# One written order for the dense experts and a two-expert chain after the attention, in place of the scheduler's

## The chip, the cores and the metric

The kernel runs on one core of a Trainium2 chip. The metric is the time of the device for one execution, in microseconds (us); the numbers before are the median of three runs and one profiled execution. TensorE is called PE below (its weight loads PEld), VectorE DVE, ScalarE ACT, GpSimd POOL; SP (SyncE) issues most of the transfers. Each engine carries out its own instructions in the order in which they stand in its queue, and waits on semaphores for the others.

## The reference, cut to what matters

The input x has 4 batches of 1024 tokens with 128 features. The network has four layers with residuals: causal softmax attention with 16 heads, a mixture of experts, linear attention with 16 heads of width 8, and the same mixture of experts again. Each layer's input is normalised first.

```python
x = x + attention_a(_layernorm(x), Wq, Wkv, Wo, bo)     # softmax, 16 heads of 64
x = x + ffn(_layernorm(x), router_w, expert_weights)
x = x + attention_b(_layernorm(x), ...)                 # cumulative sums, 16 heads of 8
x = x + ffn(_layernorm(x), router_w, expert_weights)
# ffn: 32 experts of 128x128, the two best of each token
rw = softmax(x @ router_w.T)
vals, idx = top_k(rw, 2)
w_masked = zeros_like(rw).at[tokens, idx].set(vals)
out = sum(x_flat * w_masked[:, e:e+1] @ W[e] for e in range(32))
```

All of it is in float32.

## The kernel before, in words

All tokens stay in `x_sb`, as 32 row blocks of 128 tokens (8 for each batch). The attention phase runs over batches and pairs of heads, in an order that is written out by hand (`tc.manual_schedule()` keeps the order of the program on each engine).

The mixture of experts is computed in two ways. The **two-expert chain** (`experts`, a Python generator that is advanced a piece at a time) does a whole batch sparsely: router, places by prefix sums, a scatter of the tokens' scaled rows into a buffer in DRAM (`xs_d`, indirect DMA from POOL), per group of four experts a load, transposes, matmuls and a store (`ys_d`), and then 16 gathers from DRAM (`fetch`, L449). Scatters and gathers are put in a `queue`, from which the caller takes one at a time. The chains of batches 0 to 2 run beside the attention; the last pieces of batch 2's, its 16 gathers, are left over at the attention's end. The **dense way** computes for a row block all 32 experts: 8 matmuls `pe` of 128x512 (L922), each with four experts, from the 32 resident weights `we_sb`. Of the 8 results, five are scaled and added to `x_sb` by DVE (20 instructions at L937), three (`ACT_GROUPS`) are scaled by ACT into tiles `t` (L930), which POOL adds up (L944 to L946), and DVE adds the sum (L871, in `settle`). The router's weights `w` (L892 to L912) come before: normalise, transpose, copy `xnT`, logits `pl`, softmax, two maxima, `match_replace`.

After the attention there are three stages. **Stage f** is the dense way for the last 8 row blocks (`moe("f", ...)`, two quads of four), and beside it `fill` advances the gathers that are left and `prepare(0)` and `prepare(1)`, the features of the linear attention for the first 8 row blocks (statistics, POOL's `nb_l`, ACT's `xn_l`, transposes, four projections `pj`, Exp, Sigmoid, Ln). The **linear attention** (`lin`) goes over 32 row blocks: POOL makes the products `kv`, PE sums them cumulatively (`cumulate`, `carry`), DVE multiplies and reduces (`m`, `num`), and PE projects; `ahead` advances the next `prepare`. **Stage s** is the dense way for row blocks 8 to 31 (six quads of four), and beside it `pieces` advances the chain for batch 0.

In stages f and s nothing fixes the order by hand: there the framework's scheduler decides it, from priorities and its costs, and may also draw instructions of a later stage forward between those of the linear attention, which has a written order of its own:

```python
        if turn[0] in (4, 18):
            preps.append(prepare(len(preps), pool))
        if turn[0] % 2:
            for p in preps:
                next(p, None)
```

In the dense way of before the whole router of a quad stands in the program ahead of that quad's matmuls, and `between` (that is `fill` or `pieces`) is called once before each matmul. There are 5 PSUM banks for `pe` and 3 for everything else.

Of the kernel before, what the change touches and what calls it, by code (L numbers as in the profile page):

```python
# [20 lines left out]
def hybrid_kernel(  # L21
# [107 lines left out]

    def normed_T(pool, xnp, c0, n, nm, known=None):  # L130

        mv, rstd = known or statistics(c0, n, nm)
        xn = xnp.tile([P, n, D], F32, tag=f"xn{n}", bufs=8 // n, name=f"xn_{nm}")
        xnT = xnp.tile([P, n * P], F32, tag=f"xnT{n}", name=f"xnT_{nm}")
        for c in range(n):
            nc.vector.tensor_scalar(
                xn[:, c, :], x_sb[:, c0 + c, :], mv[:, c, 0:1], rstd[:, c : c + 1],
                ALU.subtract, ALU.mult,
            )
        for g in range(0, n, 4):  # L140
            pt = pool.tile([P, 512], F32, tag="ps1", name=f"pxn_{nm}_{g}")
            for c in range(4):
                nc.tensor.transpose(pt[:, c * P : (c + 1) * P], xn[:, g + c, :], ident)
            nc.scalar.copy(xnT[:, g * P : (g + 4) * P], pt)
        return xnT
# [711 lines left out]
    TB = 12  # L857
    ACT_GROUPS = (1, 4, 6)

    def moe(nm_, store, first=0, between=None, known=(), lag=0):  # L860
        with ExitStack() as ph:
            xnp = ph.enter_context(tc.tile_pool(name=f"xnp{nm_}", bufs=2, reuse_waits="tile"))
            mp = ph.enter_context(tc.tile_pool(name=f"mp{nm_}", bufs=3, reuse_waits="tile"))
            ps_1 = ph.enter_context(tc.tile_pool(name=f"mps1{nm_}", bufs=3, space=PSUM, reuse_waits="tile"))
            ps_e = ph.enter_context(tc.tile_pool(name=f"mpse{nm_}", bufs=5, space=PSUM, reuse_waits="tile"))
            due = []

            def settle(keep):
                while len(due) > keep:
                    xs, s, done = due.pop(0)  # L870
                    nc.vector.tensor_tensor(xs, xs, s[:, :D], ALU.add)  # L871
                    if store and done is not None:
                        b, r = divmod(done, NB)
                        nc.sync.dma_start(
                            out=out_v[b, :, r : r + 4, :], in_=x_sb[:, done : done + 4, :]
                        )

            for q in range(first, NT // 4):
                nm = f"{nm_}_{q}"
                c0 = q * 4  # L880
                xnT = normed_T(
                    ps_1, xnp, c0, 4, f"m{nm}", known[q - first] if known else None
                )
                pl = ps_1.tile([P, 512], F32, tag="ps1", name=f"pl_{nm}")
                for c in range(4):
                    nc.tensor.matmul(
                        pl[:, c * E : (c + 1) * E], xnT[:, c * P : (c + 1) * P], rwT,
                        start=True, stop=True,
                    )
                plv = pl[:, : 4 * E].rearrange("p (c e) -> p c e", c=4)  # L890
                mx = small.tile([P, 4], F32, tag="mx", name=f"mx_{nm}")
                nc.vector.tensor_reduce(mx, plv, AX.X, ALU.max)  # L892
                ex = mp.tile([P, 4, E], F32, tag="ex", name=f"ex_{nm}")
                nc.vector.tensor_tensor(
                    ex, plv, mx.unsqueeze(2).to_broadcast([P, 4, E]), ALU.subtract
                )
                nc.scalar.activation(ex, ex, AF.Exp)
                sm = small.tile([P, 4], F32, tag="sm", name=f"sm_{nm}")
                nc.vector.tensor_reduce(sm, ex, AX.X, ALU.add)
                nc.vector.reciprocal(sm, sm)  # L900
                tp, rwx = top[q % 2]
                nc.vector.tensor_tensor(
                    rwx[:, :, 0:E], ex, sm.unsqueeze(2).to_broadcast([P, 4, E]), ALU.mult
                )
                m8 = small.tile([P, 4, 8], F32, tag="m8", name=f"m8_{nm}")
                for c in range(4):
                    nc.vector.max(m8[:, c, :], rwx[:, c, 0:E])
                nc.vector.tensor_copy(tp[:, :, 0:2], m8[:, :, 0:2])
                w = mp.tile([P, 4, E + 6], F32, tag="w", name=f"w_{nm}")
                for c in range(4):  # L910
                    nc.vector.match_replace(w[:, c, :], tp[:, c, :], rwx[:, c, :], 0.0)
                nc.vector.tensor_tensor(  # L912
                    w[:, :, 0:E], rwx[:, :, 0:E], w[:, :, 0:E], ALU.subtract
                )
                for c in range(4):
                    xs = x_sb[:, c0 + c, :]
                    parts = []
                    for g in range(E // 4):
                        if between:
                            between(ps_1)  # L920
                        pe = ps_e.tile([P, 512], F32, tag="e", name=f"pe_{nm}_{c}_{g}")
                        nc.tensor.matmul(  # L922
                            pe, xnT[:, c * P : (c + 1) * P],
                            we_sb[:, 4 * g : 4 * g + 4, :].rearrange("p e d -> p (e d)"),
                            start=True, stop=True,
                        )
                        if g in ACT_GROUPS:
                            t = mp.tile([P, 512], F32, tag="t", bufs=TB, name=f"t_{nm}_{c}_{g}")
                            for e in range(4):
                                nc.scalar.mul(  # L930
                                    t[:, e * D : (e + 1) * D], pe[:, e * D : (e + 1) * D],
                                    w[:, c, 4 * g + e : 4 * g + e + 1],
                                )
                            parts.append(t)
                        else:
                            for e in range(4):
                                nc.vector.scalar_tensor_tensor(  # L937
                                    xs, pe[:, e * D : (e + 1) * D],
                                    w[:, c, 4 * g + e : 4 * g + e + 1], xs,
                                    ALU.mult, ALU.add,  # L940
                                )
                    s = parts[0]
                    for t in parts[1:]:
                        nc.gpsimd.tensor_tensor(s, s, t, ALU.add)  # L944
                    nc.gpsimd.tensor_tensor(s[:, :256], s[:, :256], s[:, 256:], ALU.add)
                    nc.gpsimd.tensor_tensor(s[:, :D], s[:, :D], s[:, D : 2 * D], ALU.add)  # L946
                    due.append((xs, s, c0 if c == 3 else None))
                    settle(lag)
            settle(0)


# [96 lines left out]
    def fill(pool):  # L1048

        banks[0] = pool  # L1050
        turn[0] += 1
        if turn[0] in (4, 18):
            preps.append(prepare(len(preps), pool))
        if turn[0] % 2:
            for p in preps:
                next(p, None)
        elif turn[0] > 8:
            if queue:
                queue.pop(0)()
            for e in list(sides):  # L1060
                if next(e, "end") == "end":
                    sides.remove(e)

    turn, preps = [0], []
    moe("f", False, NT // 4 - 2, fill, known)
    for p in preps:
        for _ in p:
            pass
    assert not (sides or queue) and len(preps) == 2

    with lin as ph:

        ph.enter_context(tc.manual_schedule())
        lp = ph.enter_context(tc.tile_pool(name="lp", bufs=3))
        ps_c = ph.enter_context(tc.tile_pool(name="ps_c", bufs=1, space=PSUM))
        ps_n = ph.enter_context(tc.tile_pool(name="ps_n", bufs=1, space=PSUM))
        ps_1 = ph.enter_context(tc.tile_pool(name="ps_l", bufs=4, space=PSUM))
        AHEAD = 26

        def products(u):  # L1080

            kq, va = feats[u // G]
            k = kq[:, u % G, :P]
# [72 lines left out]
        def ahead(third):  # L1156
# [5 lines left out]
            for r in list(running):  # L1162
                if next(r, "end") == "end":
                    running.remove(r)

        kv = products(0)
        ends = []
        for u in range(NT + 4):
# [9 lines left out]
            if u < NT:  # L1178
                carry(u, kv)
                f = finish(u, m)  # L1180
                next(f)
                ends.append(f)
                kv = nkv
            ahead(3 * u + 2)

    def pieces(pool):

# [43 lines left out]
```

## Time and profile before

| what | before |
|---|---|
| runs | 2033.25 us median of 3 (2030.45 to 2037.73) |
| profiled execution: its own time | 2037.51 us |
| profiled execution: span from first to last instruction | 2035.8 us |
| mean granted PE clock | 0.975 |
| PE busy | 1890.7 us (93%) |
| DVE busy | 1482.9 us (73%) |
| ACT busy | 1234.6 us (61%) |
| POOL busy | 1139.5 us (56%) |
| DMA | 62.54 MB moved |

The page gives the busy time of each engine, the span in 40 slices with the busy share in tenths, and groups of instructions by source line. The trace is also read in stretches of time (busy time of each engine, granted clock, DMA share), as waits (who waited for whom) and as a timeline. Busy shares are averages over stages with different limits, so a stage is read from its own stretch.

### The profile page before, as it was taken

The numbers are of one execution on the slowest core, as the hardware profiler recorded it, in microseconds if no ns is written. First come the engines' busy times: TensorE is split into PE (matmuls) and PEld (weight loads), VectorE is DVE, ScalarE is ACT, GpSimd is POOL, SyncE is SP. The second block draws the span as 40 slices with busy tenths as digits, with TensorE's granted clock in tenths as the row PEclk, the third lists the DMA queues.
The fourth block names the chain that finished last, engine by engine and source line by source line (L and its number), as shares of the span: only waits on it lengthen the run. The fifth ranks groups of instructions, "written<-read, shape, count | busy, mean of one in ns | idle before, by whom it ended". The sixth has DMA issues, their size and how long they took to land.

```text
span 2035.8 us, 33636 instructions
## 1 busy us (share of the span) xinstructions
PE 1890.7 (93%) x10066; PEld 1052.5 (52%) x10066; DVE 1482.9 (73%) x4467; ACT 1234.6 (61%) x3889; POOL 1139.5 (56%) x2080
## 2 busy tenths in 40 slices
PE   6999999999999999999999999999958898987898
PEld 3555555555555655555565555556633454543443
DVE  5777776776787677778767676777547678966788
ACT  4766666676677566766766676776526466334344
POOL 3444445444665476556745854675476566655644
PEclk9999999999999999999999999999979999997999
DMA  7000000000003310000131100003230000004300
GB/s 214 1 1 1 1 1 1 1 1 1 1 13 93 92 22 10 1 1 5 54 107 45 18 1 1 1 17 111 80 82 0 0 0 1 0 1 123 101 11 11
DMA packets 111875, 62.54 MB, mean 31 GB/s; under 512 B 5552, under 2 KB 110160, under 8 KB 111568
## 3 DMA queue, kind: packets, MB, share of 16 engines
q1 hardware_dynamic: 101936, 50.43, 8.7%
q0 software_dynamic: 9472, 8.40, 2.1%
q8 instruction: 82, 1.34, 0.3%
q10 hardware_dynamic: 288, 1.57, 0.2%
q14 instruction: 97, 0.79, 0.1%
HBM read 35.60 MB, written 24.77 MB: 30 GB/s over the span
## 4 chain that ended last, share of the span: by engine, by line
PE 64%; DVE 12%; ACT 10%; POOL 9%; issue 3%; DMA 1%; ACTq 0%; SPq 0%; POOLq 0%; DVEq 0%
PE s L598 19%; PE po L704 10%; PE pt L687 10%; PE pe_s L922 6%; DVE nmx L607 5%; ACT p L632 3%; PE pw L719 3%; PE pk L547 3%; POOL x_sb L449 2%; ACT pT L691 2%; PE pe L430 2%; PE pv L561 2%; PE cum L1103 1%; ACT p L637 1%; PE pe_f L922 1%
## 5 line engine op out<-in xcount | busy, mean ns | idle before, releaser
L607 DVE TENSOR_REDUCE nmx<-s 128x2 f32<-128x1024 f32 x512 | 604.5, 1219 | 218.5 <-PE s L598 217.8
L632 ACT ACTIVATE p<-s,nmx 128x512 f32<-128x512 f32 (+3 forms) x640 | 361.2, 575 | 311.8 <-DVE nmx L607 264.5
L598 PE MATMUL s<-kT,qT 64*128 64x512 f32 x2048 | 518.0, 619 | 8.0 <-ACT p L632 4.5
L674 POOL TENSOR_SCALAR p<-p,f,ri 128x512 f32<-128x512 f32 (+3 forms) x768 | 503.8, 673 | 0.9 <-issue 0.6
L687 PEld LDWEIGHTS pt<-ident,p 128*128 128x128 f32 x2304 | 249.9, 141 | 219.1 <-issue 91.1
L687 PE MATMUL pt<-ident,p 128*128 128x128 f32 x2304 | 335.9, 282 | 24.4 <-POOL rs L652 7.1
L691 ACT COPY pT<-pt 128x512 f32<-128x512 f32 (+3 forms) x768 | 324.4, 510 | 11.9 <-PE pt L687 9.6
L656 POOL TENSOR_TENSOR rs<-rs,f 128x2 f32<-128x2 f32 x256 | 52.1, 204 | 438.5 <-ACT f L623 409.1
L704 PE MATMUL po<-pT,va 128*64 128x256 f32 (+1 forms) x2560 | 291.1, 365 | 0.6 <-DVE oT L711 0.6
L598 PEld LDWEIGHTS s<-kT,qT 64*128 64x128 f32 x2048 | 173.3, 185 | 195.4 <-issue 94.2
L637 ACT ACTIVATE p<-s,nmx 128x128 f32<-128x128 f32 x512 | 180.7, 366 | 107.3 <-DVE nmx L607 104.6
L704 PEld LDWEIGHTS po<-pT,va 128*64 128x64 f32 x2560 | 167.0, 136 | 97.2 <-issue 32.6
L922 PE MATMUL pe_s<-we_sb,xnT_ms 128*128 128x512 f32 x384 | 186.4, 630 | 22.9 <-DVE x_sb L937 16.4
L937 DVE SCALAR_TENSOR_TENSOR x_sb<-pe_s,w_s,x_sb 128x128 f32<-128x128 f32 x480 | 141.4, 343 | 19.2 <-PE pe_s L922 14.6
L645 DVE SCALAR_TENSOR_TENSOR p<-p,qtri 128x128 f32<-128x128 f32 x512 | 144.9, 310 | 7.0 <-ACT p L637 3.9
L652 POOL TENSOR_TENSOR rs<-rs 128x2 f32<-128x2 f32 x192 | 43.9, 229 | 186.7 <-DVE ri L665 186.7
L632 ACT ACTIVATION_READ_ACCUMULATOR p<-s,nmx 128x1 f32 x640 | 139.0, 217 | 0.0
L930 ACT ACTIVATE t_s<-pe_s,w_s 128x128 f32<-128x128 f32 x288 | 82.2, 369 | 92.5 <-PE pe_s L922 75.5
L922 PEld LDWEIGHTS pe_s<-we_sb,xnT_ms 128*128 128x128 f32 x384 | 72.2, 199 | 116.3 <-issue 37.4
L944 POOL TENSOR_TENSOR t_s<-t_s,t_s 128x512 f32<-128x512 f32 x48 | 60.9, 1269 | 81.4 <-ACT t_s L930 81.1
L724 DVE TENSOR_TENSOR x_sb<-pw,x_sb 128x128 f32<-128x128 f32 x128 | 36.9, 289 | 79.8 <-PE pw L719 79.7
L719 PE MATMUL pw<-wo_sb,oT 128*128 128x128 f32 x512 | 84.5, 289 | 1.8 <-DVE x_sb L724 1.0
(302 smaller groups left out, 2669.5 us busy)
## 6 DMA issues: line engine op xcount, KB each, us to landing
xs<-xs_d SPq DMA_DIRECT2D x33, 256.0 KB, 3.1
ys_d<-ys SPq DMA_DIRECT2D x33, 256.0 KB, 2.4
we<-_ffn_expert_weights_dram SPq DMA_DIRECT2D x24, 256.0 KB, 3.6
xs_d<-zero SPq DMA_DIRECT2D x2, 3008.0 KB, 17.9
we<-_ffn_expert_weights_dram SPq DMA_DIRECT2D x45, 64.0 KB, 1.8
xs_s<-xs_d SPq DMA_DIRECT2D x11, 256.0 KB, 3.6
ys_d<-ys_s SPq DMA_DIRECT2D x11, 256.0 KB, 3.4
we_sb<-_ffn_expert_weights_dram SPq DMA_DIRECT2D x4, 512.0 KB, 6.0
```

The source lines that it names most:

```text
L598: nc.tensor.matmul(st[:, h, :], self.qT[rows, self.ib * P : (self.ib + 1) * P], self.kT[rows, j * 512 : (j + 1) * 512], start=True, stop=True,
L607: nc.vector.tensor_reduce(self.nmx[:, i, :], self.s[i], AX.X, ALU.max, negate=True)
L632: nc.scalar.activation(self.p[h][:, at : at + m * P], self.s[i][:, h, : m * P], AF.Exp, bias=bias, accum_out=self.rs[:, i, h : h + 1],)
L637: nc.scalar.activation(self.p[h][:, at + m * P : at + (m + 1) * P], self.s[i][:, h, m * P : (m + 1) * P], AF.Exp, bias=bias,)
L645: nc.vector.scalar_tensor_tensor(d, d, 1.0, qtri, ALU.mult, ALU.mult, accum_out=self.rs[:, 2, h : h + 1])
L674: nc.gpsimd.tensor_scalar(w, w, self.f[:, i, h : h + 1], self.ri[:, h : h + 1], ALU.mult, ALU.mult,)
L687: nc.tensor.transpose(pt[:, c * P : (c + 1) * P], self.p[h][:, (g + c) * P : (g + c + 1) * P], ident,)
L691: nc.scalar.copy(self.pTs[h][:, g : g + m, self.col : self.col + P], pt[:, : m * P].rearrange("p (c i) -> p c i", c=m),)
L704: nc.tensor.matmul(po[h * DH : (h + 1) * DH, c0:256], va[:, jb, h, :], pTs[h][:, jb, c0:], start=(jb == 0), stop=(jb == n - 1),)
L719: nc.tensor.matmul(pw[:, :P], oTs[i][:, c * P : (c + 1) * P], wo_sb[:, pr, :], start=(i == 0), stop=(i == len(prs) - 1),)
L922: nc.tensor.matmul(pe, xnT[:, c * P : (c + 1) * P], we_sb[:, 4 * g : 4 * g + 4, :].rearrange("p e d -> p (e d)"), start=True, stop=True,)
L937: nc.vector.scalar_tensor_tensor(xs, pe[:, e * D : (e + 1) * D], w[:, c, 4 * g + e : 4 * g + e + 1], xs, ALU.mult, ALU.add,)
```

## The change

`moe` and `normed_T` go, and two functions take their place. `routed` is a generator that gives a quad's statistics, normalisation, transposes, logits and routing weights in small pieces, and leaves `xnT` and `w` in `ready`. `dense` goes over the quads; after each matmul and its scaling it advances the router of the *next* quad by one piece and calls `beside(turn)`. From the attention's end on everything is under `manual_schedule`, so the order of the program is the order on each engine. POOL's adds of the scaled tiles stand directly after the second and third tile, and DVE adds a block's sum while it is at matmul 3 of the third block after it (`settle(2)`).

Beside stage f, `fill` advances `prepare(0)` and `prepare(1)` in turn and takes one gather in each four matmuls; while the router of the first quad is written, `prepare(0)` is advanced a piece for each of its pieces. The router of stage s's first quad is written into the last steps of the linear attention, two pieces in each. Beside stage s, `pieces` takes one scatter or gather in each two matmuls, and advances batch 0's chain in five of eight turns, and in three of eight in its part with the loads, transposes and matmuls (`passing`). The pools of the linear attention reuse their buffers tile by tile. The instructions themselves are the same.

```diff
-    def moe(nm_, store, first=0, between=None, known=(), lag=0):
...
+    ctx.enter_context(tc.manual_schedule())
+    rp = ctx.enter_context(tc.tile_pool(name="rp", bufs=2, reuse_waits="tile"))
+    ready = {}
+    def routed(q, nm, pool, known=None):
...
+        for c in range(4):
+            nc.vector.tensor_scalar(
+                xn[:, c, :], x_sb[:, c0 + c, :], mv[:, c, 0:1], rstd[:, c : c + 1],
+                ALU.subtract, ALU.mult,
+            )
+            if c == 1:
+                yield
+        yield
+        yield
+        yield
+        pt = pool.tile([P, 512], F32, tag="ps1", name=f"pxn_{nm}")
+        for c in range(4):
+            nc.tensor.transpose(pt[:, c * P : (c + 1) * P], xn[:, c, :], ident)
+        nc.scalar.copy(xnT, pt)
...
+        ready[q] = xnT, w
+    def dense(nm_, qs, store, pool, mp, ps_e, known, beside):
...
+        for i, q in enumerate(qs):
+            xnT, w = ready.pop(q)
+            nxt = iter(())
+            if i + 1 < len(qs):
+                nxt = routed(qs[i + 1], f"{nm_}_{qs[i + 1]}", pool, known[i + 1])
+            for c in range(4):
...
+                for g in range(E // 4):
...
+                        parts.append(t)
+                        if len(parts) > 1:
+                            nc.gpsimd.tensor_tensor(parts[0], parts[0], t, ALU.add)
...
+                    if g == 3:
+                        settle(2)
+                    next(nxt, None)
+                    beside(turn)
+                    turn += 1
...
+            for _ in nxt:
+                pass
+        settle(0)
...
-        if turn[0] % 2:
-            for p in preps:
-                next(p, None)
-        elif turn[0] > 8:
...
+    def on():
+        for e in list(sides):
+            if len(queue) <= 4 and next(e, "end") == "end":
+                sides.remove(e)
...
+        def fill(turn):
+            next(preps[turn % 2], None)
+            if turn % 4 == 3:
+                if queue:
+                    queue.pop(0)()
+                on()
+        qs = list(range(NT // 4 - 2, NT // 4))
+        for _ in routed(qs[0], f"f_{qs[0]}", ps_f, known[0]):
+            next(preps[0], None)
+        dense("f", qs, False, ps_f, mp, ps_e, known, fill)
...
+            if u == NT - 8:
+                first = routed(qs[0], f"s_{qs[0]}", ps_1)
+            next(first, None)
+            next(first, None)
...
-    moe("s", True, NB // 4, pieces, lag=3)
+    def pieces(turn):
+        if turn % 2 and queue:
+            queue.pop(0)()
+        if turn % 8 in ((0, 3, 6) if passing[0] else (0, 2, 3, 5, 6)):
+            on()
...
+        dense("s", qs, True, ps_s, mp, ps_e, [None] * len(qs), pieces)
```

## The prediction

> **What bounds the kernel now.** I read the page first, then busy time by stage, then the waits and the timeline of the stages that the change reorders. The page's slices (50.9 us each) come first: PE is full from slice 2 to slice 29, and loses its nines in the last eleven.
>
> ```profile
> PE   6999999999999999999999999999958898987898
> PEclk9999999999999999999999999999979999997999
> ```
>
> So the attention phase, up to about 1484 us, is bounded by PE. The built program has there the same instructions in the same order on every engine (but for one gather, below), so I price it at nothing. What follows has three stages: dense experts "f" on the last 8 row blocks (1484 to 1594), linear attention (to 1786), dense experts "s" on 24 row blocks with batch 0's two-expert chain (to the end). Busy time by stage (columns: stretch, length, PE, PEld, DVE, ACT, POOL, granted clock, DMA share, GB/s):
>
> ```profile
> 1786.00:2036.00 250.00, 213.03 (x621) 101.28 (x621) 183.96 (x707) 102.63 (x337) 135.92 (x154) 0.92 0.18 50
> 1484.00:1594.00 110.00, 78.98 (x176) 34.26 (x176) 67.30 (x242) 53.02 (x155) 73.35 (x82) 0.83 0.18 37
> 1594.00:1786.00 192.00, 169.85 (x532) 96.45 (x532) 157.87 (x376) 98.94 (x241) 123.13 (x94) 0.94 0.00 1
> ```
>
> No engine fills f (PE 79 of 110) or s (PE 213 of 250, part of it at a lower clock). In stretches of 10 us the holes are local:
>
> ```profile
> 1500.00:1510.00 10.00, 1.63 (x4) 0.73 (x4) 4.85 (x16) 1.65 (x4) 9.34 (x11) 0.50 0.22 27
> 1820.00:1830.00 10.00, 7.93 (x28) 4.27 (x28) 3.89 (x12) 2.33 (x7) 8.74 (x17) 1.00 0.00 0
> 1830.00:1840.00 10.00, 4.12 (x4) 1.00 (x4) 8.15 (x41) 3.75 (x12) 7.09 (x11) 0.66 0.14 40
> 1960.00:1970.00 10.00, 9.56 (x23) 4.02 (x22) 9.42 (x37) 5.29 (x19) 4.99 (x5) 1.00 0.00 1
> ```
>
> The last line is s without the chain: PE at 9.56 of 10, DVE at 9.42. That is what the stage can do; the dense matmuls of L922 alone, in stretches of 20 us (PE, PEld), say the same:
>
> ```profile
> 1820.00:1840.00 20.00, 9.68 (x16) 3.21 (x16) 0.83 0.07 20
> ...
> 1960.00:1980.00 20.00, 19.04 (x44) 7.87 (x42) 1.00 0.05 14
> ```
> The timeline shows what opens the hole in f (start, duration, engine, line; in brackets idle time and who ended it):
>
> ```profile
> 1501.45 0.18 DVE L978 BATCH_NORM_AGGREGATE mv_l<-st_l 128x2 f32<-128x6 f32 x1 [8.59 <-POOL nb_l L985]
> 1510.67 1.26 ACT L992 ACTIVATE xn_l<-x_sb,nb_l,rstd_l 128x128 f32<-128x128 f32 x3 [5.52 <-POOL nb_l L986]
> 1513.00 8.42 PE L922 MATMUL pe_f<-we_sb,xnT_mf 128*128 128x512 f32 x12 [7.32 <-ACT t_f L930]
> ```
>
> The scheduler drew statistics of a third linear-attention tile forward. DVE waits for their buffer behind POOL's 16 gathers, the routing weights stand behind that on DVE, then ACT waits for POOL, and PE, five banks ahead, stops. In s the long waits are also of order:
>
> ```profile
> POOL t_s L944 <- ACT t_s L930: 81.1, 35, 11.7
> ACT t_s L930 <- PE pe_s L922: 75.5, 59, 8.0
> ACT xsT_s L443 <- PE pxs_s L441: 22.3, 11, 8.1
> ```
>
> **The change part by part.** No instruction is added or removed on any engine: the counts by operation and shape agree, names of tiles aside. So all of it is order, and every step is an interval of before against the sums of its engines.
>
> *Stage f.* The 16 gathers (L449) leave their block: one falls into the attention's end, where POOL idles 9.28 us before rstd_mf; 15 stand between the POOL adds of t_f, one in four matmuls. The head gets longer: ACT's copy of xnT now stands behind the four xn_l of `prepare(0)`, which wait for POOL's nb_l. By the timeline's rows, DVE's mean and variance are done at 1484.4 + 4x0.27 + 4x0.45 = 1487.3; four POOL operations (0.73, 1.05, 0.75, 0.77) end at 1490.6; xn_l 1.65 and two copies 1.2 end at 1493.5; four projections at 1.25 of ACT each end at 1498.5; Exp and its sum 2.15 and the router's Exp 0.31 at 1501.0; the DVE part of the router 3.6 with L1032 between: first scaled add near 1505 against 1502.1. But there it goes on, where before PE stood until 1513.0. From 1505: PE 64 matmuls x 0.86 (two records at a pitch of 0.43) + 3.4 of projections, 1.2 of transposes, 1.1 of logits = 61; DVE 160 x 0.295 (their pitch where they run on) + 13 (second router and its normalisation 4.1, one tile's statistics and y 3.0, two kq 3.5, eight sums 2.3) = 60; POOL t_f 30.7, ln and kq 10, nb chain 3.3, gt 1.3, and 15 gathers at 1.27 (the pitch of a gather with another operation behind it) to 1.87 (gather to gather) = 19 to 28, so 64 to 73, and about 5 of waiting. POOL is last and ends near 1578; then the first kv follows, which before started at 1594.3. Step: -15, from -2 (POOL waits for ACT as it did before, 16.0) to -20.
>
> *Linear attention.* PE, POOL and ACT keep their order; DVE loses what the scheduler had put between: 8+20 statistics at 0.28, 24 aggregates at 0.18 and four ve_ms, 5.1 together, 17.0 in all, and gains some 3.5 of the first router. In the stretch 1660 to 1765 PE waits 12.0 for m from DVE ahead of the carry. PE works 22.5 of each 25.1 us there (four blocks), so no more than 2.5 per group can come back: -6, from 0 (the chain runs over POOL's kv and ln in the same groups) to -12.
>
> *Seam to s.* Before, num ended at 1782.9, and the first scaled add came at 1792.5, because transpose, logits and router stood after the last block. Now they stand in its last steps: o, transpose, copy, product 2.3, the rest of the router 1.9: first add near 1787.5. -5, from 0 (a transposed block not ready holds PE's queue) to -6.
>
> *Stage s.* From the first scaled add to the last, 1792.5 to 2031.5, it took 239. The stage's pace without chain is 172 records of L922 in 1940 to 2020 (41, 44, 43 and 44 in four stretches), two for each of 8 matmuls, so 10.75 row blocks in 80 us: 7.44 each. The chain adds PE time of 26 (pe_s L430 14.6, pxs_s 8.0, the rest logits and counts) and spreads over some 170 of 192 turns (34 pieces at five in eight 54, 16 scatters at one in two 32, 15 pieces with loads and matmuls at three in eight 40, 16 gathers 32, the rest waiting for the queue), 21 row blocks: 7.44 + 26/21 = 8.7. DVE: 480 x 0.295 + router and chain as now, plus 12.6 of statistics moved here from linear attention, less 2 of the first router, 191 in all against PE's 191 at full clock, so there is no slack between them. 21x8.7 + 3x7.44 = 205. Added waits: each crossing from POOL to DVE or PE in the chain now holds what is behind it, the scaled adds on DVE and the matmuls on PE: the nine prefix operations, then u, then pos; then wt and the count matmul. Before, such crossings cost DVE 4.9 (pos), 3.0 (big) and 2.2 (mx). I take 13 for all, between 0 and 34 (no gain): 218, step -21. SP keeps its loads one chain step ahead, some 5 us against 3.6 to land; POOL's scatters (0.98 and a memset 0.13) overrun a row block by about 1 us, which `settle(2)`, more than two row blocks behind, covers; without that cover DVE pays 4. The end (last sum, store) stays.
>
> A rule against the change: the Trainium skill, "PSUM — Partial Sum Buffer", section "Engine vs sequencer instructions", calls the queues of ScalarE, VectorE and GpSimdE strictly first in, first out, so a written order passes each late step on in full; the 8.59 above agrees. By the rule alone I would double the 13, and the forecast below would be 13 higher, 1999; by the rows it stays.
>
> Sum: -15 -6 -5 -21 = -47. Against the profiled execution's own 2037.51 that is 1990.5; the median of the runs shown is 4.3 lower, so 1986.
>
> On the clock: PE's granted clock was 0.50 in 1500 to 1510 and 0.66 in 1830 to 1840, each at a hole, and 1.00 where PE is fed; the sums of f and s use the pitch at 1.00 and need no term for it.
>
> **Rivals.** (A, forecast) as summed; 0.70. (B) Stage s stays at 239, because DVE with 191 of work and PE with the same feed each other over five banks and the moved statistics fill the holes; f, linear attention and the seam give -26: 2007 on the scale of the median. For it: DVE's 9.42 beside PE's 9.56. Against it: 1820 to 1830, where DVE does 3.89 and PE 7.93. 0.16. (C, slower) The chain at fixed turns holds PE's queue at each step, so that all of it runs like 1820 to 1870, where PE was busy 34.2 of 50: 21 blocks at (6.88+0.42+1.15)/0.68 = 12.4, and 22: 283, +44; with -26, 2051. It decides from s = 265, PE below 0.74 of it. Against it: the longest waits of DVE and PE for the chain in s are 4.9 (pos) and 4.0 (pxs_s), and DVE was busy for 27.3 of those 50. 0.11. (D) The order only swaps holes, POOL's 73 with its waits ends f no earlier and s stays: within 6 of 2033; 0.03.
>
> **How the numbers follow.** The steps' far ends give -2+0+0+0 and -20-12-6-34 = -72, so 1961 at the best; 1965 leaves little out. Above, B and D are taken in up to 2030, and C is left out. Within 0.3% (6 us) a measurement cannot tell this kernel from no change. Faster 0.86 (A and B), same 0.03 (D), slower 0.11 (C).
>
> **What would show it.** Right: PE busy again by 1506 and not idle to 1513; gathers spread over f; first kv near 1578; linear attention some 186 long; about 218 from first to last scaled add, clock near 1.00. Wrong: DVE or PE waiting over 4 us on POOL's u, pos or cnt several times; ACT's t_f waiting on POOL; s above 239.

## The result and the profile after

The changed kernel takes 2051.03 us (median of 4 runs, 2047.43 to 2052.64), the kernel before 2033.24 in the same session (4 runs, 2030.45 to 2037.73). The ratio is 1.0083, 95% interval 1.006 to 1.0106: slower by 0.8%, where the forecast was 1986. The profiled execution took 2047.43, with a span of 2045.7 (before 2037.51 and 2035.8).

The page's slices, 51.1 us each (PE, DVE and granted clock, from the page of the changed kernel):

```profile
PE   6999999999999999999999999999877989878886
DVE  5777776776787767678767677776569788988888
PEclk9999999999999999999999999999989999989989
```

PE still loses its nines in the end, now in the last slices most of all (8886, before 7898). DVE's digits there are eights and nines. Busy time by stage (f, linear attention, s; columns as in the prediction):

```profile
1484.00:1585.00 101.00, 77.61 (x176) 31.08 (x176) 78.45 (x234) 53.77 (x155) 72.02 (x66) 0.91 0.15 28
1585.00:1777.00 192.00, 171.09 (x549) 96.93 (x550) 157.09 (x348) 97.51 (x235) 117.18 (x87) 0.96 0.00 1
1777.00:2042.00 265.00, 215.38 (x606) 99.67 (x604) 231.22 (x740) 102.82 (x342) 142.34 (x177) 0.91 0.18 50
```

In s DVE is busy for 231 of 265; before it was 184 of 250, for the same instructions but for some 12 of statistics (of the router, L853, L854 and L857, and of the chain), which the scheduler had put into the linear attention. Stretches of 10 us say that this is no matter of a few holes:

```profile
1820.00:1830.00 10.00, 3.31 (x7) 0.97 (x6) 9.37 (x53) 1.44 (x6) 3.98 (x4) 0.79 0.00 0
1830.00:1840.00 10.00, 7.14 (x18) 4.09 (x19) 6.44 (x18) 2.58 (x8) 4.03 (x7) 0.69 0.00 0
2010.00:2020.00 10.00, 8.44 (x18) 3.28 (x19) 9.12 (x24) 3.69 (x14) 4.38 (x5) 1.00 0.04 11
2020.00:2030.00 10.00, 8.76 (x20) 3.21 (x19) 9.12 (x24) 3.42 (x12) 4.73 (x6) 1.00 0.00 0
```

The last two lines are s without the chain and without the router. Before, PE was at 9.56 in a stretch without the chain; now it is at 8.4 to 8.8, and DVE at 9.12 with only 24 instructions in 10 us. The dense matmuls alone (L949, 20 us, PE and PEld) fell from 19.04 to this:

```profile
2000.00:2020.00 20.00, 16.64 (x36) 6.07 (x35) 1.00 0.10 27
```

The timeline of DVE and POOL names the two things that DVE spends more time on:

```profile
2010.47 1.35 DVE L931 TENSOR_TENSOR x_sb<-x_sb,t_s 128x128 f32<-128x128 f32 x1
2011.74 7.75 DVE L966 SCALAR_TENSOR_TENSOR x_sb<-pe_s,w_s,x_sb 128x128 f32<-128x128 f32 x20
2010.41 1.26 POOL L963 TENSOR_TENSOR t_s<-t_s,t_s 128x512 f32<-128x512 f32 x1 [1.77 <-ACT t_s L957]
```

The 20 adds of one row block stand in a row, each into the slice that the one before it wrote: 7.75/20 = 0.388 each. The sum of L931, 0.28 where nothing lies beside it, lies beside a POOL addition and lasts as long as that. The trace of before had both pitches of the add side by side, and the prediction averaged over them:

```profile
1967.25 0.28 DVE L871 TENSOR_TENSOR x_sb<-x_sb,t_s 128x128 f32<-128x128 f32 x1
1967.44 2.35 DVE L937 SCALAR_TENSOR_TENSOR x_sb<-pe_s,w_s,x_sb 128x128 f32<-128x128 f32 x6
1970.93 3.45 DVE L937 SCALAR_TENSOR_TENSOR x_sb<-pe_s,w_s,x_sb 128x128 f32<-128x128 f32 x13 [1.14 <-PE pe_s L922]
```

2.35/6 = 0.39, and 3.45/13 = 0.265. Counted over all of s, where an add directly follows another and starts less than 0.1 behind its end: before, 282 start 0.259 behind the one ahead of them and 64 start 0.384 behind it; after, 14 start 0.267 behind it and 360 start 0.384 behind it. The group lines of s, DVE (busy, mean ns), show how an average hides it; before:

```profile
L937 DVE SCALAR_TENSOR_TENSOR x_sb<-pe_s,w_s,x_sb 128x128 f32<-128x128 f32 x480 | 141.4, 343 | 19.2 <-PE pe_s L922 14.6
L871 DVE TENSOR_TENSOR x_sb<-x_sb,t_s 128x128 f32<-128x128 f32 x24 | 8.9, 370 | 6.6 <-POOL t_s L946 6.5
```

and after:

```profile
L966 DVE SCALAR_TENSOR_TENSOR x_sb<-pe_s,w_s,x_sb 128x128 f32<-128x128 f32 x480 | 166.3, 349 | 26.1 <-PE pe_s L949 10.1
L931 DVE TENSOR_TENSOR x_sb<-x_sb,t_s 128x128 f32<-128x128 f32 x24 | 15.9, 671 | 0.0
```

The mean of one add hardly moves (343 to 349 ns). The busy time does, by 24.9: before, 480 x 0.343 = 165 of durations filled 141, so they overlapped; after, they don't. And of the 26.1 that DVE stands idle ahead of them, only 10.1 is a wait that the profile names. The other 16.0 are short gaps, of 0.04 for most adds, so the adds hold DVE for some 182 of the stage.

Where the time went, by first and last scaled adds of the two profiles: s begins at 1777.6 in place of 1792.5 (14.9 gained, 26 forecast), and takes 263.6 to the start of the last add in place of 238.7 (24.9 lost, 21 gain forecast). Together 10.0; the spans differ by 9.9.

### The profile page after: what moved, and what is told of

Same layout as the page of the kernel before. It is cut to its first block, busy times and chain, and to the rows that moved or that the text cites. A ratio compares the mean times of both kernels' runs of the same rounds, so it can differ in the third digit from the quotient of the medians.

```text
span 2045.7 us, 33584 instructions
## 1 busy us (share of the span) xinstructions
PE 1892.4 (93%) x10066; PEld 1048.2 (51%) x10066; DVE 1539.8 (75%) x4467; ACT 1232.6 (60%) x3889; POOL 1137.9 (56%) x2080
## 3 DMA queue, kind: packets, MB, share of 16 engines
q8 instruction: 82, 1.34, 0.3%
## 4 chain that ended last, share of the span: by engine, by line
PE 61%; DVE 18%; ACT 9%; POOL 7%; issue 4%; DMA 1%; SPq 0%; ACTq 0%; DVEq 0%; POOLq 0%
PE s L581 19%; PE po L687 10%; PE pt L670 10%; DVE nmx L590 6%; DVE x_sb L966 5%; PE pe_s L949 4%; ACT p L615 4%; PE pw L702 3%; PE pk L530 3%; ACT pT L674 2%; PE cum L1152 2%; PE cum L1144 2%; PE pe L413 2%; ACT p L620 1%; PE pv L544 1%
## 5 line engine op out<-in xcount | busy, mean ns | idle before, releaser
L949 PE MATMUL pe_s<-we_sb,xnT_s 128*128 128x512 f32 x384 | 191.5, 639 | 17.7 <-ACT t_s L957 16.1
L966 DVE SCALAR_TENSOR_TENSOR x_sb<-pe_s,w_s,x_sb 128x128 f32<-128x128 f32 x480 | 166.3, 349 | 26.1 <-PE pe_s L949 10.1
L957 ACT ACTIVATE t_s<-pe_s,w_s 128x128 f32<-128x128 f32 x288 | 81.7, 368 | 85.8 <-PE pe_s L949 80.6
L949 PEld LDWEIGHTS pe_s<-we_sb,xnT_s 128*128 128x128 f32 x384 | 72.5, 202 | 115.4 <-issue 46.8
```

The costliest lines, as they stand in the source:

```text
L949: nc.tensor.matmul(pe, xnT[:, c * P : (c + 1) * P], we_sb[:, 4 * g : 4 * g + 4, :].rearrange("p e d -> p (e d)"), start=True, stop=True,)
L966: nc.vector.scalar_tensor_tensor(xs, pe[:, e * D : (e + 1) * D], w[:, c, 4 * g + e : 4 * g + e + 1], xs, ALU.mult, ALU.add,)
```

## The experiments

Theory T: a scaled add that follows its own predecessor costs 0.38 us on DVE in place of 0.27, and this makes DVE the bound of s. Theory W (rival C of the prediction, in a milder form): the chain's pieces at fixed products hold the queues of PE and DVE. Theory P: DVE is held up by POOL's additions. Times "first to last add" below are of stage s, from the first scaled add to the start of the last, in the profile of each run. Runs that leave out a part of the work, and the two with rows added at the end, were executed once each. Those two contain the changed kernel's stage s as it is, and took 264.7 and 264.4 for it against 263.6, so a difference of a few microseconds in s is more than chance.

**Pairs of row blocks.** Two row blocks at once, their adds alternating:

```python
for c0 in (0, 2):
    cs = (c0, c0 + 1)
    for g in range(E // 4):
        ...                       # one matmul for each c of cs
        for e in range(4):
            for c in cs:
                xs = x_sb[:, q * 4 + c, :]
                nc.vector.scalar_tensor_tensor(xs, pes[c][...], w[...], xs, ALU.mult, ALU.add)
```

> The written order stays, but the dense experts take two row blocks at once: matmul, four ACT scales or four DVE adds of block c, then the same of block c+1, and the DVE adds of the two alternate (c, c+1, c, c+1), so that no add follows the one that wrote its own operand. Theory T (an add that follows its own predecessor costs 0.38 us in place of 0.28): 640 adds x 0.1 = 64 us less work on DVE; stage s, where DVE is busy over 9 of 10 us, falls from 264 to about 215, f from 80 to about 75 (POOL bounds it there), the time to 1985 to 2005. Theory W (the chain's pieces at fixed turns hold the queues of PE and DVE): the holes stay, s between 250 and 264, the time 2035 to 2051. Theory P (VectorE is held up by POOL's additions, not by its own predecessors): the pitch of the adds stays at 0.35, the time 2035 to 2051.

Measured: 2034.11, ratio to before 1.0001 (0.9992 to 1.0011): 17 less than the changed kernel, not 46 to 66. The adds' busy time in s fell from 166.3 to 130.4, 0.272 each, so T is right on the price and P wrong; first to last add is 245.4. DVE's idle time before the adds rose to 38.0, 37.7 of it waiting for PE, probably because nothing is ready for DVE behind two products for ACT in a row. Something else sets the pace now.

**The dependence cut, the order kept.**

```diff
-                                xs, pe[:, e * D : (e + 1) * D],
+                                away[:, e, :], pe[:, e * D : (e + 1) * D],
                                 w[:, c, 4 * g + e : 4 * g + e + 1], xs,
```

> The order of the changed kernel, instruction for instruction; only the scaled adds write to a spare tile in place of the slice that they read, so none depends on the one before it (the experts' sum is left out of the result). Theory T: pitch 0.28, s about 215, the time 1985 to 2005, like the paired version. Theory P or W: pitch 0.35 to 0.39 and 2035 to 2051. If the cost were in the order and not in the dependence (for instance four adds in a row out of one bank), this one stays at 2051 while the paired one gains.

Measured: 2022.4, first to last add 237.9. The group's line in s, with the same number of instructions in the same order:

```profile
L968 DVE SCALAR_TENSOR_TENSOR away<-pe_s,w_s,x_sb 128x128 f32<-128x128 f32 x480 | 130.9, 341 | 30.1 <-PE pe_s L951 29.7
```

Neither expectation holds, but the order is kept and the pitch is not, so the cost lies in the dependence. It alone costs the changed kernel 2051.03 - 2022.4 = 28.6, more than the 17.8 by which it lost. But 17 to 37 of the gain that T promised are missing.

**Without the chain; and without both.** In the first run batch 0's chain is left out of s:

```diff
-    for b, r in enumerate((room,)):
-        sides.append(experts(b, f"s{b}", banks, queue, r, came))
```

> The changed kernel without batch 0's two-expert chain in stage s (that part of the work is left out). Theory T: DVE still bounds the stage with 20 adds x 0.38 + 0.35 + router and statistics 1.0 = 8.9 a row block, 24 x 8.9 = 214, so 50 less than 264. Theory W: without the chain nothing holds the queues, the pace is the 7.4 of the kernel before, 24 x 7.4 = 178, so 86 less.

Measured: 2012.74, first to last add 227.8, longer than both expectations and nearer to T (214) than to W (178). DVE is busy for 206.7 of it, and some 15 more are the short gaps between adds, so it bounds the stage here. The second run has both edits:

> The dependence cut as before (the experts' sum is left out) and the two-expert chain left out of stage s besides. The run with the cut alone took 238 from the first to the last scaled add, the one without the chain alone 228. Theory T plus W: without both, nothing is left but PE and DVE feeding each other, 7.4 to 7.7 a row block, 24 blocks 178 to 185, the time 1963 to 1972; so the chain costs 53 to 60 once the adds are at 0.26, of which 26 are PE's own work and some 30 are waits of the written order. Rival (the stage's order itself is slow, chain or not: 20 adds, sums and router in a fixed sequence): 8.3 or more a block, s over 200, the time over 1985.

Measured: 1967.02, and 179.8 from first to last add, 7.5 a row block. The four runs make a table (first to last add of s):

| | with the chain | without | the chain costs |
|---|---|---|---|
| adds depend | 263.6 | 227.8 | 35.8 |
| adds cut loose | 237.9 | 179.8 | 58.1 |
| the dependence costs | 25.7 | 48.0 | |

Neither theory alone holds: the two costs hide each other in part. Either alone costs 48 or 58, both together 263.6 - 179.8 = 83.8, where their sum would be 106. 480 adds at 0.385 - 0.262 would be 59 of DVE's time; beside the chain, more than half of it costs nothing.

**The pitch by itself.** Behind the changed kernel's last sum, rows of 24 adds out of one PSUM bank, into `into[:, k % n, :]` for n = 1 to 4, and a row of plain sums into one slice:

> The changed kernel, and behind its last sum five rows of 24 instructions on an otherwise idle chip: scaled adds of 128x128 out of one PSUM bank into one slice, into two, three and four slices in turn, and plain sums of two SBUF operands into one slice. Theory T: 0.38 per add into one slice, about 0.27 for two, three and four; the plain sum too is slower into one slice than the 0.28 of a single one. Theory P: with POOL idle all four rows run at about 0.27.

The timeline of DVE there:

```profile
2047.44 9.24 DVE L1265 SCALAR_TENSOR_TENSOR into<-pe_own,one,into 128x128 f32<-128x128 f32 x24
2056.99 6.29 DVE L1265 SCALAR_TENSOR_TENSOR into<-pe_own,one,into 128x128 f32<-128x128 f32 x24
2063.73 6.29 DVE L1265 SCALAR_TENSOR_TENSOR into<-pe_own,one,into 128x128 f32<-128x128 f32 x24
2070.59 6.29 DVE L1265 SCALAR_TENSOR_TENSOR into<-pe_own,one,into 128x128 f32<-128x128 f32 x24
2077.06 7.79 DVE L1272 TENSOR_TENSOR plain<-plain,x_sb 128x128 f32<-128x128 f32 x24
```

One slice: 9.24/24 = 0.385. Two slices: 0.262, and three or four bring nothing more. An add lasts 0.35 into one slice and 0.34 into several, so an independent one starts 0.08 ahead of its predecessor's end, a dependent one 0.04 behind it. Plain sums into one slice: 0.325 each.

**POOL beside it.** Four such rows into four slices, POOL idle or with eight sums of 128x512:

> The changed kernel, and behind its last sum four rows of 24 VectorE instructions into four slices in turn: scaled adds out of PSUM with POOL idle, the same beside eight POOL sums of 128x512, then plain sums of two SBUF operands with POOL idle and beside eight POOL sums. Theory P (POOL's work holds VectorE up): the row of scaled adds beside POOL is slower than 6.3. If only instructions with both operands in SBUF are held (as sums of 1.3 to 2.4 us beside POOL's suggest): scaled adds 6.3 both times, plain sums near 24 x 0.27 = 6.5 alone and about 10, as long as POOL's sums last, beside it.

```profile
2051.88 6.29 DVE L1275 SCALAR_TENSOR_TENSOR into<-pe_own,one,into 128x128 f32<-128x128 f32 x24
2058.34 6.29 DVE L1275 SCALAR_TENSOR_TENSOR into<-pe_own,one,into 128x128 f32<-128x128 f32 x24
2058.98 9.91 POOL L1270 TENSOR_TENSOR big<-big 128x512 f32<-128x512 f32 x8
2073.71 13.71 DVE L1280 TENSOR_TENSOR into<-into,x_sb 128x128 f32<-128x128 f32 x24
2074.39 10.26 POOL L1270 TENSOR_TENSOR big<-big 128x512 f32<-128x512 f32 x8
```

The scaled adds, with one operand in PSUM, run as fast beside POOL as alone: P falls for them. The plain sums, both operands in SBUF, take 13.71 where 24 x 0.27 = 6.5 was estimated, more than the 10 expected. One by one, eight of them last 1.34, each about as long as the POOL sum that it meets. The others last 0.28 and start 0.20 apart, so a row alone would take some 4.9 (estimate from that pitch). The third row, meant to run alone, met the tail of POOL's first eight and took 8.29; its last 20 sums start 0.20 apart too. This agrees with the Trainium skill, "SBUF — State Buffer", section "SBUF: two separate sides", by which VectorE with two SBUF inputs and a GpSimd operation that reads SBUF exclude each other. In the changed kernel it is the smaller part: L931 15.9 in place of 8.9, so 7 of the 52 by which DVE's busy time from first to last add grew (230.3 against 178.6).

**Counter-test: the cut in the kernel before.** The same edit in the scheduler's kernel:

> The kernel before, with its scheduler, and the scaled adds writing to a spare tile (the experts' sum is left out). A counter-test of theory T: the scheduler of the kernel before had already put adds of two row blocks, or other VectorE work, between those that depend on each other (480 adds in 141.4 busy, 0.295 each), so there is little to gain: 480 x 0.033 = 16 of DVE's work in s, of which PE lets at most some 5 through: 2025 to 2034, against the 29 that the changed kernel gained from the same edit. If the cut gains 25 here too, the dependence does not tell the two kernels apart.

Measured: 2041.65 (one run; before 2035.16). It was expected between 2025 and 2034, and got no gain at all, though the adds' busy time in s fell from 141.4 to 130.3: with other dependences the scheduler drew up another order, in which DVE once waited 11.7 for POOL's sum. Since the order changed with the edit, this run doesn't show what the dependence costs the kernel before; it shows only that the edit gains nothing there.

**Two sums for a row block.** The dependence can be broken with nothing left out. Adds of odd experts go into a tile of their own:

```diff
+                            into = odd if e % 2 else xs
                             nc.vector.scalar_tensor_tensor(
-                                xs, pe[:, e * D : (e + 1) * D],
-                                w[:, c, 4 * g + e : 4 * g + e + 1], xs,
+                                into, pe[:, e * D : (e + 1) * D],
+                                w[:, c, 4 * g + e : 4 * g + e + 1], into,
```

and POOL, or DVE in `settle`, adds `odd` in.

> Two sums for a row block: the adds of even experts go into the slice, those of odd experts into a tile of their own (its first one is a product without a sum), so two adds in a row never depend on each other; POOL adds the two up at the end of its fold, one operation of 128x128, 0.46 each, more per row block. The order is otherwise the changed kernel's. Theory T: like the run with the dependence cut, 2018 to 2030; f, which POOL bounds with the gathers, gets up to 8 x 0.46 = 3.7 longer. If the order of blocks were the cause: 2045 to 2055.

> The same two sums, but VectorE adds them up where it adds POOL's part: one more instruction of 0.28 to 0.33 per row block on DVE, none on POOL. Theory T: the run with the cut, 2022, plus at most 32 x 0.33 = 10: 2020 to 2033.

Measured: 2029.61, ratio 0.9988 (0.9979 to 0.9998), and 2028.64, ratio 0.998 (0.9971 to 0.999). Both inside what T gave, some 22 less than the changed kernel. Next, four products for ACT in s (`groups = (1, 3, 5, 7)`) with DVE adding up:

> Two sums added up by VectorE as before, and in stage s four of eight products go to ScalarE (1, 3, 5, 7) in place of three. DVE loses 24 x 4 x 0.262 = 25, ACT gains 24 x 4 x 0.285 = 27 (105 to 132), POOL 24 x 1.27 = 30 (143 to 173 of some 238). If DVE still sets the pace of s with the chain: 10 to 20 faster than with three products, 2005 to 2018. If what is left are waits of the chain on POOL's crossings, the same or slower: 2022 to 2040.

Measured: 2043.37, ratio 1.0054 (1.0038 to 1.0071), 15 slower than with three, beyond both expectations. DVE no longer set the pace, waiting 48.0 for PE in s; POOL's busy time rose to 172.8 of 259. That the fuller POOL delays the chain's crossings is likely, but was not shown.

**The chain spaced out.** Two sums by DVE, and empty pieces in the chain between a step on POOL or a DMA and the step on PE or DVE that needs it, here the first:

```diff
+        for _ in range(3):
+            yield
         pc = banks[0].tile([P, 512], F32, tag="ps1", name=f"pc_{nm}")
         nc.tensor.matmul(
```

(for batch 0's chain in s alone), with two more ahead of `pos`, one ahead of `row`, three behind the second load of tokens. In the run with the cut, this is what such a crossing does (timeline of PE and DVE):

```profile
1825.74 1.33 PE L281 MATMUL pc_s<-cnta,onesq 128*128 128x288 f32 x2 [6.07 <-POOL cnta L275]
1830.16 1.13 DVE L968 SCALAR_TENSOR_TENSOR away<-pe_s,w_s,x_sb 128x128 f32<-128x128 f32 x4 [4.39 <-PE pe_s L951]
```

PE stands 6.07 with all the dense matmuls behind it, and DVE then waits 4.39 for PE.

> Two sums added up by VectorE (2028.6 alone), and empty pieces between a step of batch 0's chain on POOL or a DMA and the step on PE or DVE that needs it: three ahead of the count matmuls, two ahead of pos, one ahead of row and wt, three behind the second loads of tokens. Everything else keeps its fixed product. Theory W (what is left over the pace of 7.4 a row block is the written order's waits at these crossings): PE's waits for cnta (6.4) and for the tokens (4.5) and DVE's for u (3.7) shrink to about nothing, 10 to 14 us less, 2014 to 2020; the chain ends some 17 us later, still ahead of the last product. If the chain's cost lies in its own work on the engines: 2026 to 2031, no gain.

Measured: 2016.12, ratio 0.9899 (0.9881 to 0.9917), 12.5 less than with the two sums alone, and first to last add 231.5 in place of 244.8. With the two sums alone, the list of waits in s (total, times, longest) has these three, and the spaced version's has none of them:

```profile
PE pc_s L281 <- POOL cnta L275: 6.4, 1, 6.4
PE pxs_s L424 <- DMA xs_s<-xs_d: 4.5, 1, 4.5
DVE pos_s L323 <- POOL u_s L320: 3.7, 1, 3.7
```

This version beats both kernels. The 12.5 compares runs of two sessions, in which the kernel before took 2031.71 and 2035.16; measured against the kernel before, the gain is 16.0, and in stage s it is 13.3. The same spacing on the changed kernel, adds still dependent:

> The changed kernel with the empty pieces of the spaced version alone; the scaled adds still depend on each other (one sum). Theory T with W behind it: VectorE at 0.385 an add is the later of the two, busy 9.1 to 9.4 of 10 us already, so most of PE's waits for cnta and the tokens lie beside VectorE's work: 0 to 6 less than 2051, 2045 to 2051. If the two costs add up, as the sum of the prediction takes them: 10 to 14 less, 2037 to 2041.

Measured: 2044.29, ratio 1.0045 (1.0028 to 1.0062): 6.7 less, between the two expectations. Against the kernel before of its session it is 9.0 less, and stage s takes 255.1, 8.5 less. So the spacing brings 54 to 64% of what it brought with two sums, by whichever of the three measures. That fits theory T, by which a part of PE's waits lies beside DVE's work.

**Two more tries on the spaced version.**

> The spaced version with the two sums added up by POOL in place of VectorE (24 x 0.34 = 8 less on DVE in s, 24 x 0.46 = 11 more on POOL, which works 144 of 233 there), and the router's transposes three products later in s, since PE waits 8.6 for the normalised blocks of VectorE, ten times. DVE is busy 9.7 or more of 10 us in most stretches of the spaced version, so if DVE sets its pace: 6 to 12 less, 2004 to 2012 where the spaced version took 2016. If POOL's additional sums hold the chain: 2014 to 2022.

Measured: 2023.49, ratio 0.9944 (0.9931 to 0.9958), 7 slower than the spaced version where a gain was expected. One of its two edits alone:

> The spaced version (two sums added up by VectorE, 2016) with the router's transposes three products later in s and nothing else: this part of the last run alone. If PE's 8.6 of waits for the normalised blocks were on the path: 2008 to 2013. If VectorE sets the pace: 2014 to 2019. If the slower last run (2023.5) came from the later transposes and not from POOL's sums: 2020 to 2026.

Measured: 2016.21, ratio 0.9902 (0.9886 to 0.9919): no change from 2016.12. So the later transposes are worth nothing, and it was POOL's additional sums that cost 7. Where they cost it is not shown: s takes 231.8 and 230.4 in the two profiles, and the first kv behind f comes at 1587.5 and 1584.8.

## Why the prediction was wrong

**The failed step: stage s, "DVE: 480 x 0.295 + router and chain as now".** 0.295 was the busy time of the add divided by its count in the scheduler's order. It was carried into an order in which nearly every add follows its own predecessor; there the pitch is 0.384. DVE's busy time from first to last add, put at 191, came to 230.3 of 263.9. The adds are 25 of the 39 more, and the 16 of short gaps come on top, so DVE became the bound. With the order kept and the dependence cut, DVE is busy for 195.8, and the stage is 25.7 shorter (table). It could have been seen beforehand: the two pitches stand beside each other in the trace of before, and the changed kernel's program writes the 20 adds of a row block one behind the other into one slice.

**The second term: the added waits of the chain, "I take 13".** With the adds cut loose, the chain costs 58.1, which is 32 beyond PE's own 26, near the upper end of 34. That makes s 238, not 218. So the same order without the dependence gives what the scheduler gave (238.7), the length that rival B named, though not for B's reason. The rule set against the change in the prediction, a strict queue that passes each late step on, was the better guide there; by it the 13 became 26. Spacing takes 13.3 of the stage back, so that much was waits at the four crossings. What the rest is stays open: the chain also adds 28 to DVE's work (195.8 against 167.8). And the term depends on what it is added to: with the adds as they are, the chain costs 35.8, only 10 beyond PE's 26, which is less than the 13.

Together: forecast 1990.5 for the profiled execution; 11 less gained ahead of s (26 against 14.9), 20 more for the chain, 25.7 of the dependence: 2047.2. It took 2047.43. That this adds up proves little, since the last two terms split one measured difference. Split the other way, by the table's other row and column, the dependence is 48.0 and the chain 3 less than forecast. Either way the dependence is the larger term.

**Stage f: the first kv came 9.0 earlier (1585.3), where -15 was forecast.** The head was right: first scaled add at 1504.7, forecast near 1505; PE stopped 4.86 for `xn_f` of DVE, until 1506.8, and ran through from 1508.8 to 1513. That POOL ends f last was right too: it is busy 9.1 to 9.5 of each 10 us from 1520 to 1580. From the first add to the first kv (the stretch, one of POOL's waits in it, and two neighbours in POOL's timeline):

```profile
1504.72:1585.31 80.59, 64.00 (x142) 24.84 (x142) 72.31 (x203) 41.26 (x127) 68.61 (x61) 0.95 0.10 13
L1016 POOL TENSOR_TENSOR rstd_l<-mv_l,epsn 128x4 f32<-128x4 f32 x1 | 0.2, 201 | 5.3 <-DVE mv_l L1011 5.3
1530.38 1.56 POOL L432 DMA_INDIRECT x_sb<-ys_d,row  x1 [0.15 <-issue]
1531.47 1.24 POOL L977 TENSOR_TENSOR t_f<-t_f 128x256 f32<-128x256 f32 x1
```

POOL's work of 68.6 lies within the forecast 64 to 73. The term that was short is "about 5 of waiting": 12.0 of the 80.6 are idle, 5.3 of them in one wait for statistics from DVE and 1.2 for DVE's sum ahead of kv, the rest in short gaps. Rows of POOL can't be added up here: an addition that stands behind a gather starts 0.47 ahead of the end of the gather's row and lasts 0.5 longer than another (128x256: 1.25 against 0.72), so the two rows overlap. The cut shows that DVE's longer adds cost f little: its last add came 10.0 earlier there (1574.3), the first `num` of the linear attention only 2.2.

**Linear attention and seam: right in direction, short in size.** From the first kv to the end of the last num: 186.2 against 188.6, so -2.4, where -6 was forecast. The wait for m from DVE ahead of the carry, which was to shrink, did not: it is 12.7 in the same 105 us, in place of 12.0 (the weight load's wait; PE's own is 9.1 in place of 8.5). The seam took 6.2 from there to the first scaled add against 9.6, so -3.4 for -5.

**The clock.** "1.00 where PE is fed" held for single stretches (2010 to 2030 above), not for s: granted 0.91 from the first add to the last, before 0.94. Nor did it hold throughout before: from 1930 to 1940 PE was busy 9.28 of 10 us at a granted 0.72. With the dependence cut it is 0.95 in s, and 1.00 without the chain besides.

**Rival C** named 2051 and the time was 2051, which was luck: it asked for chain stretches with PE at 0.68, and for PE below 0.74 of s; PE is busy for 215 of 265, 0.81. Without the dependence the same chain at the same products gives 238, on the faster side.

## What to carry to other kernels

The time of an instruction in a row can depend on its neighbour: where an order is changed, look up in the trace the pitch behind its own predecessor and behind another, and count in the built program which one the new order has. A scheduler's interleaving may be hiding a dependence; when the order is written by hand, alternate accumulators. In a written order, put several steps between a product of a slow engine or DMA and the first use on an engine that others wait for, and ask which engine is the later one there: the same spacing was worth 13.3 of stage s with two sums and 8.5 with dependent adds. Two such costs can hide each other, so that only a run with both removed shows what each is worth.

## What the runs showed of the hardware

- VectorE's 128x128 scaled add out of PSUM: 0.385 per instruction into one slice, 0.262 into two or more in turn; it lasts 0.35 and 0.34. The Trainium skill, "VectorE: DVE Perf Modes", section "The DRAIN you can't avoid", states that the next operation does not start until the pipe has emptied, and adds that one that is not held starts earlier. Here dependent adds start 0.04 behind the end of the one before, and independent ones 0.08 ahead of it.
- VectorE's sums of two 128x128 operands in SBUF start 0.325 apart into one slice and 0.20 apart into four in turn.
- A VectorE sum of two SBUF operands that meets a POOL sum of 128x512 lasts about as long as that (1.34 in place of 0.28); POOL's eight took 10.26 in place of 9.91. Scaled adds with an operand in PSUM are not held up (6.29 in both cases).
- On POOL, as the profile records it, the row of a gather into `x_sb` and the row of the addition behind it overlap by 0.47, and that addition lasts 0.5 longer (128x512: 1.78 against 1.27), so a mean over such rows (1.59 in f) is not the price of the addition.
